# Moving statistics, weight loads and a write order in a two-layer convolution kernel on one core

## The chip, the cores and the metric

The kernel runs on one core of a Trainium2 chip. The metric is the device time of one execution in microseconds, as a median of several runs. Profiles are of one execution each; their spans start with the first instruction. Engines are named as the profile names them: PE (TensorE), DVE (VectorE), ACT (ScalarE), POOL (GpSimd), SP (the queue that issues most DMAs).

## The reference

The input x has four images of 16 channels and 256 x 256 pixels, float32. Two layers are added to it, each after a group normalization `_gn` (eight groups of two channels: subtract the mean, divide by the root of the variance plus 1e-5).

Layer 0 computes 400 = 16 x 25 logits per pixel by a 3 x 3 convolution of the normalized image, takes a softmax over the 25 of each channel, and uses these as weights for the 5 x 5 neighbours of the pixel in the normalized image:

```
out = conv(x_n, conv_w) + conv_b
weights = softmax(out.reshape(N, C, 25, H, W), axis=2)
x1 = x + sum over u of unfold(x_n)[:, :, u] * weights[:, :, u]
```

Layer 1 normalizes x1 in the same way, and adds to it a 3 x 3 convolution of silu of the normalized x1 and of eight cubic B-spline features of it, plus a bias. Layer 1 therefore needs the mean and variance of x1 for every image and group, which exist only when layer 0 has finished that image.

## The kernel before

**Prologue** (the code in the pool block before `layer0`). Each of the eight half images of x (128 rows, 16 channels) is loaded by `load_x` (the DMA at L413); the halves of image 0 stay in `held`. DVE takes statistics with bn_stats (L524, L526), ACT squares the same data (L533) and PE sums the squares (L536), for a bound on the logits. `group_stats` turns the statistics into mean and rstd; the power -0.5 is taken on POOL (L152, `rstd_x`), and DVE copies the result into `nrm[b]` (L544, L545), which holds rstd and -mean x rstd per group. Image 0 is then normalized by `normalize`, a generator that is advanced between the bn_stats of the later images: ACT writes normalized rows (L317, L330), PE transposes (L352), DVE and ACT write a plain copy, a rounded copy and the rest (L345, L360), and SP's queue writes all of that to scratch memory in HBM (`hs`, `hst`, `hsl`; the DMAs at L278 and L292). `normalize` first writes zero borders into that scratch (L250, L256, L257, twelve DMAs per image). The weights of both layers are loaded on SP's queue: `wr`, `wnr` (L421, L428, L433) for layer 0, and `sw`, `ss`, `bw` (L440, L442, L447: 27 + 3 + 1 DMAs) for layer 1. POOL multiplies sw by ss (L488) and rearranges `wr` and `wnr` (L465, L466). `norm_tiles` makes the buffers of `normalize` and clears them whole on POOL (L231, L233); it is called in the prologue and again in layer 0.

**Layer 0** goes over 64 strips of 128 rows x 32 columns, each in eight steps of four columns. In a step PE computes 400 logits for each column (L780, L784), ACT takes exp into `e[:, 0]` (L803), POOL multiplies with the neighbours into `e[:, 1]` (L808), and DVE sums both over the 25 neighbours into `nd` (L685): `nd[:, 0]` is the denominator and `nd[:, 1]` the weighted sum, both laid out column by column with the 16 channels innermost. There are four e buffers. A small scheduler, `after(k, f)` and `step()`, runs follow-up work k steps later: `seed` (ACT, Ln and Exp, L698 and L699), `divide` (DVE, L703 to L705, one Newton step in PSUM tile `r`), `apply` (POOL, L711: the weighted sum, which `divide` leaves with a minus sign, is subtracted from x in `xc`, which gives x1), and after every fourth strip `statistics` (DVE, eight bn_stats of 256 elements, L719) and `store` (a DMA on ACT's queue, L729). Beside the strips of images 0 to 2 the next image is normalized by `normalize`, one piece per step, on ACT, PE, DVE and SP's queue.

**Between the layers.** `scales(b)` turns the statistics of x1 (`st1[b]`) into the scale and bias of layer 1 for image b, in small steps on DVE, PE, ACT and POOL (L179 to L213). For images 0 and 1 these steps run in the last image of layer 0, for images 2 and 3 between units of layer 1.

**Layer 1** goes over 64 units of 16 rows. ACT makes distances and powers (L931, L161 to L164) and silu (L913), DVE the spline features (L156, L165 to L167) into `ring`, PE the convolution (L977, L985, L993), and DVE adds the bias (L960).

What sets the order: [...]The tile framework chooses the order from the order of the calls and from what each needs; `in_order` fixes it inside the layers, and `marks` lets the first work of layer 1 on ACT and SP slip between the last strips of layer 0, with the first silu (L913) behind all of layer 0's ACT work.

Of the kernel before, what the change touches and what calls it, by code (L numbers as in the profile page):

```python
# [11 lines left out]
F32 = mybir.dt.float32  # L12
F32R = mybir.dt.float32r
AF = mybir.ActivationFunctionType
ALU = mybir.AluOpType
AX = mybir.AxisListType
# [17 lines left out]
def conv_preact_kernel(  # L34
# [12 lines left out]
    nc = tc.nc  # L47
    B, C, H, W = x.shape
    G = 8
    GC = C // G  # L50
    P = 128
    NH = H // P
# [3 lines left out]
    PAD = K // 2  # L56
    HP = H + 2 * PAD
    NS = 8
    EPS = 1e-5
    SW = 32  # L60
# [3 lines left out]
    CX = 128  # L64
    JG = 4
    LAG = 1
    RP = P + 2
# [12 lines left out]
    const = ctx.enter_context(tc.tile_pool(name="const", bufs=1))  # L80
# [3 lines left out]
    hst = [[dram.tile([C, CT], F32, name=f"hst{b}_{h}") for h in range(NH)] for b in range(B)]  # L84
# [5 lines left out]
    ones = const.tile([P, P], F32, name="ones")  # L90
    nc.vector.memset(ones, 1.0 / P)
    mhalf = const.tile([P, G], F32, name="mhalf")
# [13 lines left out]
    gsel_sb = const.tile([P, G], F32, name="gsel_sb")  # L106
# [8 lines left out]
    KT = 6 * C + 1  # L115
# [9 lines left out]
    for r in range(RT):  # L125
        p = SROWS.index(r + 1) * C
# [1 line left out]

    edge = const.tile([P, 5], F32, name="edge")
    stat1 = ctx.enter_context(tc.tile_pool(name="stat1", bufs=1))  # L130
    st1 = [const.tile([P, G, NH * (W // CX), 6], F32, name=f"st1_{b}") for b in range(B)]

    def group_stats(pool, psum, st, name):

# [36 lines left out]
    def scales(b, psum):  # L171


        def small(n, name):
            return stat1.tile([P, n], F32, name=f"{name}_{b}", tag=f"{name}{b % 2}")

        mv = stat1.tile([P, G, 2], F32, name=f"mv_{b}", tag=f"mv{b % 2}")
        for g in range(G):
            nc.vector.bn_aggr(mv[:, g, :], st1[b][:, g].rearrange("p n s -> p (n s)"))  # L179
        yield  # L180
        ps = psum()[:, 0:G]
        nc.tensor.matmul(ps, lhsT=ones, rhs=mv[:, :, 0], start=True, stop=True)
        yield
        mean, d, rstd = small(G, "mean"), small(G, "d"), small(G, "rstd")
        q = stat1.tile([P, 6], F32, name=f"q_{b}", tag=f"q{b}")
        nc.vector.tensor_sub(d, mv[:, :, 0], ps)
        nc.vector.tensor_mul(mean, gsel_sb, ps)
        nc.vector.reduce_sum(q[:, 1:2], mean, AX.X)
        yield
        nc.scalar.activation(d, d, AF.Square)  # L190
        yield
        ps = psum()[:, 0:G]
        nc.tensor.matmul(ps, lhsT=ones, rhs=d, start=True, stop=False)
        nc.tensor.matmul(ps, lhsT=ones, rhs=mv[:, :, 1], start=False, stop=True)
        yield
        nc.vector.tensor_scalar(rstd, ps, EPS, None, ALU.add)  # L196
        yield
        nc.gpsimd.tensor_tensor(rstd, rstd, mhalf, ALU.pow)  # L198
        nc.gpsimd.tensor_mul(rstd, rstd, gsel_sb)
        yield  # L200
        nc.vector.reduce_sum(q[:, 0:1], rstd, AX.X)
        nc.vector.tensor_scalar(q[:, 1:2], q[:, 1:2], q[:, 0:1], -1.0, ALU.mult, ALU.mult)
        for k in range(2):
            nc.vector.tensor_scalar(q[:, 2 + k : 3 + k], q[:, k : k + 1], 2.5, None, ALU.mult)
        yield
        ps = psum()[:, 0:2]
        nc.tensor.matmul(
            ps, lhsT=sel.rearrange("p c s -> p (c s)"), rhs=q[0:C, 2:4], start=True, stop=True
        )
        yield  # L210
        nc.vector.tensor_copy(q[:, 4:5], ps[:, 0:1])
        nc.vector.tensor_add(q[:, 5:6], ps[:, 1:2], ub)
        sc[b] = tuple(q[:, k : k + 1] for k in (0, 1, 4, 5))  # L213
        yield
# [2 lines left out]


    nrm = [const.tile([P, 2, G], F32, name=f"nrm{b}") for b in range(B)]
    NIM = 3  # L220

    def norm_tiles(prep):


        xps = [prep.tile([P, QC, W + 2 * PAD], F32, name=f"xp{h}", bufs=1) for h in range(NH)]
        tts, his, los = [
            [prep.tile([P, NH, QG, RP], d, name=f"{v}{n}", bufs=1) for n in range(2)]
            for v, d in (("tt", F32), ("hi", F32R), ("lo", F32R))
        ]
        for t in (*tts, *xps):  # L230
            nc.gpsimd.memset(t, 0.0)  # L231
        for t in (*his, *los):
            nc.gpsimd.memset(t.bitcast(F32), 0.0)  # L233
        return prep, xps, tts, his, los

    zero = const.tile([PAD * C, max(RP, NST * SP)], F32, name="zero")
# [2 lines left out]
    zpad = const.tile([P, QC, PAD], F32, name="zpad")  # L239
    nc.vector.memset(zpad, 0.0)  # L240

    def normalize(b, ptr, tiles, held=None, copier=None):

        prep, xps, tts, his, los = tiles
        copier = copier or nc.scalar.copy
        for e in (0, HP - PAD):
            for r in range(PAD):
                nc.sync.dma_start(  # L250
                    hs[b][:, e + r].rearrange("s c w -> c s w"),
                    zero[0:C, 0 : NST * SP].rearrange("c (s w) -> c s w", s=NST),
                )
        for h in range(NH):
            for w in (0, (W + 1) * RP):
                nc.sync.dma_start(hst[b][h][:, w : w + RP], zero[0:C, 0:RP])  # L256
                nc.sync.dma_start(  # L257
                    hsl[b][h][:, :, w : w + RP].rearrange("c t r -> (c t) r"), zero[:, 0:RP]
                )

# [116 lines left out]
        for q in range(C // QC):  # L377
            ahead = rows(q + 1) if q + 1 < C // QC else iter(())
# [15 lines left out]
    with tc.tile_pool(name="prep0", bufs=2) as prep, tc.tile_pool(  # L394
        name="pre", bufs=1
    ) as pre, tc.tile_pool(
        name="xin", bufs=3
    ) as xin, tc.tile_pool(name="stat", bufs=2) as stat, tc.tile_pool(
        name="pstat", bufs=1, space=PSUM
    ) as pstat, tc.tile_pool(name="ptr0", bufs=3, space=PSUM) as ptr0:  # L400

        tiles = norm_tiles(prep)
        held = [pre.tile([P, C, W + 2 * PAD], F32, name=f"held{h}") for h in range(NH)]
# [15 lines left out]
        for dj in range(3):  # L419
            v = conv_wt[dj].rearrange("(d c) n -> c d n", d=3)  # L420
# [5 lines left out]
        v = conv_wt[2, 2 * C : 3 * C]  # L426
# [8 lines left out]
        sw = pre.tile([P, 3, 9, nm], F32, name="sw")  # L435
        ss = pre.tile([P, 3, 9, nm], F32, name="ss")
        for d in range(3):
            dc = slice(d * C, (d + 1) * C)
            for k in range(9):
                nc.sync.dma_start(sw[:, d, k], spl_w[dc, k])  # L440
            v = spl_s[dc]
            nc.sync.dma_start(  # L442
                ss[:, d],
                bass.AP(tensor=v.tensor, offset=v.offset, ap=[v.ap[0], [0, NS], [1, 9 * nm]]),
            )
        bw = pre.tile([nm, 9, nm], F32, name="bw")
        nc.sync.dma_start(bw, base_w)  # L447

        ups = pstat.tile([P, 1], F32, name="ups", tag="hps")
        nc.tensor.matmul(  # L450
            ups, lhsT=ubrow.rearrange("p c s -> p (c s)"), rhs=onec[0:1], start=True, stop=True
# [63 lines left out]
        ahead = iter(())  # L515
        for b in range(B):
            st = stat.tile([P, G, NH * (GC if b == 0 else 1), 6], F32, name=f"st0_{b}", tag=f"st0{min(b, 1)}")
            for hf in range(NH):
                n = b * NH + hf
                t = loaded.pop(0)  # L520
# [22 lines left out]
            mean, rstd = group_stats(stat, pstat, st, f"x{b}")  # L543
            nc.vector.tensor_copy(nrm[b][:, 0], rstd)  # L544
            nc.vector.scalar_tensor_tensor(nrm[b][:, 1], mean, -1.0, rstd, ALU.mult, ALU.mult)  # L545
            ms = stat.tile([P, 2], F32, name=f"ms_{b}", tag="ms")
            nc.vector.tensor_mul(mean, mean, mean)
            nc.vector.tensor_reduce(ms[:, 0:1], mean, AX.X, ALU.add)
# [8 lines left out]
            if b == 1:  # L557
                prepare1()
            if b == 0:
                ahead = normalize(0, ptr0, tiles, held, nc.vector.tensor_copy)  # L560
                next(ahead)
        for _ in ahead:
            pass
# [39 lines left out]
    def layer0(shift):  # L603
# [4 lines left out]
        with tc.tile_pool(name=f"prep{arm}", bufs=2) as prep, tc.tile_pool(  # L608
# [5 lines left out]
        ) as plog, tc.tile_pool(name=f"prc{arm}", bufs=1, space=PSUM) as prc:  # L614
            ans = [imp.tile([KT, CI * RP], F32R, name=f"an{n}{arm}", bufs=1) for n in range(NIM)]
            for t in ans:
                v = t.bitcast(F32)
                nc.vector.memset(v, 0.0)
                for r in (4 * C, 6 * C):
                    nc.vector.memset(v[r : r + 1], 1.0)  # L620
            tiles = norm_tiles(prep)
            strips = [(b, hf, s) for b in range(B) for hf in range(NH) for s in range(NST)]
            nci = SW // CI
# [49 lines left out]
            def after(k, f, *args):  # L673

                later.append([k, partial(f, *args)])
# [26 lines left out]
            def divide(n, nd, xc, r):  # L702
                nc.vector.tensor_mul(nd[:, 0], nd[:, 0], r)  # L703
                nc.vector.scalar_tensor_tensor(r, nd[:, 0], 2.0, r, ALU.subtract, ALU.mult)  # L704
                nc.vector.tensor_mul(nd[:, 1], nd[:, 1], r)  # L705
                after(LAG + 3, apply, n, nd, xc)

            def apply(n, nd, xc):
                w0 = strips[n][2] * SW % CX
                v = xc[:, :, w0 : w0 + SW]  # L710
                nc.gpsimd.tensor_sub(v, v, nd[:, 1].rearrange("p j c -> p c j"))  # L711
                if w0 + SW == CX:
                    after(2, statistics, n, xc)

            def statistics(n, xc):
                b, hf, s = strips[n]
                k = hf * (W // CX) + s * SW // CX
                for g in range(G):
                    nc.vector.bn_stats(  # L719
                        st1[b][:, g, k, :],  # L720
                        xc[:, g * GC : (g + 1) * GC, :].rearrange("p c w -> p (c w)"),
                    )
                after(2, store, n, xc)

            def store(n, xc):
                b, hf, s = strips[n]
# [104 lines left out]
    def layer1(arm, last, marks):  # L831
# [3 lines left out]
        with ExitStack() as pools:  # L835
# [135 lines left out]
            def outputs(n, sx):  # L971
# [27 lines left out]
                waiting.append((b, u, yp))  # L999

            more = chain(*(
                scales(b, lambda: pstat.tile([P, 8], F32, name=f"ps{arm}", tag="ps"))
                for b in range(2, B)
            ))
            for half in range(2):
# [90 lines left out]
```

## Time and profile before

| | us |
|---|---|
| three runs | 3112.22, 3113.82, 3114.83 |
| profiled execution | 3113.9, span 3112.0 |
| DVE busy | 3010.4 (97%) |
| PE busy | 2845.3 (91%) |
| ACT busy | 2083.5 (67%) |
| POOL busy | 1938.2 (62%) |

The prologue lasts to about 144 us, where the first product of layer 0 starts on POOL; layer 0 to about 2103 us, where DVE ends its last sum; the rest is layer 1. A share over the whole span mixes the three: POOL is at work in layer 0 and nearly idle in layer 1, ACT the other way round. Section 2 of the page shows it in 40 slices, each digit the busy tenths of some 78 us:

```profile
DVE  6689999999999999999999999999999999999997
ACT  6466655456564465555444444458999999999996
POOL 2289999999999999999999999990000001000000
```

A group of instructions reads as line, engine, operation, output and inputs, shape, number; then busy time and mean nanoseconds of one; then how long the engine idled ahead of it and what ended that.

### The profile page before, as it was taken

How to read it: one execution, taken by the hardware profiler on the slowest of the kernel's cores; microseconds unless marked ns; L12 is line 12 of the kernel's file. 1: busy time of each engine (PE TensorE's matmuls, PEld its weight loads, DVE VectorE, ACT ScalarE, POOL GpSimd, SP SyncE). 2: the span in 40 equal slices, each digit the busy share in tenths (PEclk: the TensorE clock that was granted, in tenths of full speed). 3: DMA queues.
4: the chain of work that ended last, by engine and by line, in shares of the span. 5: the costliest groups of instructions: out<-in, count | busy, mean ns of one | idle time of the engine just before them, and what ended most of it. 6: DMA issues, size and time to landing. Idle time of an engine off the chain costs nothing.

```text
span 3112.0 us, 40438 instructions
## 1 busy us (share of the span) xinstructions
PE 2845.3 (91%) x14776; PEld 1494.9 (48%) x14776; DVE 3010.4 (97%) x1733; ACT 2083.5 (67%) x2107; POOL 1938.2 (62%) x659
## 2 busy tenths in 40 slices
PE   3489999999999999999899999976999999999999
PEld 2356656656565566566565665641232223222222
DVE  6689999999999999999999999999999999999997
ACT  6466655456564465555444444458999999999996
POOL 2289999999999999999999999990000001000000
PEclk7699999999999999999999999998999999999999
DMA  7978878778877778788676666659999889999994
GB/s 222 309 206 232 241 207 224 194 212 223 239 218 214 204 198 234 215 223 231 186 192 168 167 177 180 166 135 199 193 196 195 197 193 192 194 196 197 193 197 92
DMA packets 356530, 626.34 MB, mean 201 GB/s; under 512 B 45298, under 2 KB 222692, under 8 KB 340452
## 3 DMA queue, kind: packets, MB, share of 16 engines
q1 hardware_dynamic: 323300, 606.88, 78.0%
q10 hardware_dynamic: 33024, 16.78, 1.9%
q8 instruction: 121, 1.98, 0.3%
q14 instruction: 85, 0.70, 0.1%
HBM read 513.95 MB, written 104.24 MB: 199 GB/s over the span
## 4 chain that ended last, share of the span: by engine, by line
DVE 69%; PE 11%; ACT 6%; issue 6%; DMA 5%; SPq 2%; POOL 0%; DVEq 0%; ACTq 0%; POOLq 0%
DVE nd L685 48%; PE lg L780 5%; PE yp L977 4%; DVE ta L166 3%; DVE ta L165 3%; DVE tb L166 3%; DVE tb L165 3%; DVE ring L167 2%; DMA xin<-in_x_dram 2%; PE lg L784 1%; DVE st L719 1%; DVE tb L156 1%; DVE r L704 1%; DMA sx<-x1s 1%; DVE nd L703 1%
## 5 line engine op out<-in xcount | busy, mean ns | idle before, releaser
L780 PE MATMUL lg<-wm,am 128*128 128x400 f32 x4096 | 1750.2, 508 | 122.5 <-ACT e L803 108.2
L808 POOL TENSOR_TENSOR e<-e,u 128x1600 f32<-128x1600 f32 x512 | 1788.8, 3536 | 69.4 <-ACT e L803 68.2
L685 DVE TENSOR_REDUCE nd<-e 128x128 f32<-128x3200 f32 x512 | 1747.5, 3476 | 23.3 <-POOL e L808 23.2
L803 ACT ACTIVATE e<-lg 128x800 f32<-128x800 f32 x1024 | 815.8, 836 | 896.6 <-DVE nd L685 762.7
L784 PE MATMUL lg<-wn,an 97*128 97x400 f32 x2048 | 1359.3, 664 | 0.1
L780 PEld LDWEIGHTS lg<-wm,am 128*128 128x128 f32 x4096 | 766.7, 194 | 449.4 <-ACT e L803 159.2
L977 PE MATMUL yp<-ring,wt 128*32 128x512 f32 x6144 | 737.9, 594 | 53.8 <-POOL ring L948 35.5
L784 PEld LDWEIGHTS lg<-wn,an 97*128 97x128 f32 x2048 | 391.1, 191 | 311.9 <-issue 15.7
L977 PEld LDWEIGHTS yp<-ring,wt 128*32 128x32 f32 x6144 | 210.9, 108 | 571.1 <-issue 454.0
L894 POOL MEMSET sx<- 16x256 f32 x8 | 2.4, 302 | 718.5 <-PE yp L985 278.6
L993 PE MATMUL yp<-sl,ws 64*32 64x512 f32 x1536 | 176.5, 588 | 0.0
L167 DVE SCALAR_TENSOR_TENSOR ring<-ta,ta 128x2048 f32<-128x2048 f32 (+1 forms) x64 | 147.9, 2310 | 2.5
L167 DVE SCALAR_TENSOR_TENSOR ring<-tb,tb 128x2048 f32<-128x2048 f32 x64 | 145.7, 2276 | 2.6
L166 DVE TENSOR_TENSOR ta<-ta,ta 128x2048 f32<-128x2048 f32 (+1 forms) x64 | 147.3, 2301 | 0.1
L166 DVE TENSOR_TENSOR tb<-tb,tb 128x2048 f32<-128x2048 f32 x64 | 145.3, 2271 | 0.0
L913 ACT ACTIVATE sl<-sx,q 64x2048 f32<-64x2048 f32 x64 | 133.5, 2085 | 0.3 <-DMA sx<-x1s 0.3
L164 ACT ACTIVATE ta<-ta 128x2048 f32<-128x2048 f32 (+1 forms) x64 | 123.2, 1925 | 2.0
L164 ACT ACTIVATE tb<-tb 128x2048 f32<-128x2048 f32 x64 | 120.5, 1883 | 0.8 <-POOL sx L894 0.6
L711 POOL TENSOR_TENSOR xc<-xc,nd 128x512 f32<-128x512 f32 x64 | 98.8, 1544 | 11.9 <-DVE nd L705 11.9
L198 POOL TENSOR_TENSOR rstd<-rstd,mhalf 128x8 f32<-128x8 f32 x4 | 7.5, 1866 | 158.0 <-DVE rstd L196 158.0
L993 PEld LDWEIGHTS yp<-sl,ws 64*32 64x32 f32 x1536 | 48.8, 106 | 116.2 <-issue 115.9
L931 ACT ACTIVATE xta<-xta,q 128x4096 f32<-128x4096 f32 (+4 forms) x23 | 83.7, 3640 | 0.0
(171 smaller groups left out, 1917.2 us busy)
## 6 DMA issues: line engine op xcount, KB each, us to landing
am<-hst SPq DMA_DIRECT2D x512, 194.6 KB
u<-hs SPq DMA_DIRECT2D x320, 288.0 KB
an<-hsl SPq DMA_DIRECT2D x512, 129.8 KB
xta<-x1s SPq DMA_DIRECT2D x40, 1024.0 KB
xtb<-x1s SPq DMA_DIRECT2D x40, 1024.0 KB
xtc<-x1s SPq DMA_DIRECT2D x40, 1024.0 KB
am<-hst SPq DMA_DIRECT2D x256, 129.8 KB
sx<-x1s SPq DMA_DIRECT2D x248, 128.0 KB
```

The source lines that it names most:

```text
L164: nc.scalar.activation(s1, r1, AF.Square, scale=2.0)
L165: nc.vector.scalar_tensor_tensor(s2, t, 2.0, s2, ALU.subtract, ALU.mult)
L166: nc.vector.tensor_mul(s1, s1, r1)
L167: nc.vector.scalar_tensor_tensor(f, s2, 0.0, s1, ALU.min, ALU.subtract if given else ALU.add)
L685: nc.vector.tensor_reduce(nd[:, :, j : j + JG, :], e.rearrange("p t j m c d -> p t j c m d"), AX.XY, ALU.add,)
L780: nc.tensor.matmul(lg[:, i, :NL], lhsT=am[:, o : o + P], rhs=wm.rearrange("p m c d -> p (m c d)"), start=True, stop=False,)
L784: nc.tensor.matmul(lg[:, i, :NL], lhsT=an[:, o : o + P], rhs=wn.rearrange("p m c d -> p (m c d)"), start=False, stop=True,)
L803: nc.scalar.activation(ev, lg[:, :, :NL], AF.Exp)
L808: nc.gpsimd.tensor_tensor(e[:, 1].rearrange("p j m c d -> p j (m c) d"), e[:, 0].rearrange("p j m c d -> p j (m c) d"), uv, ALU.mult,)
L913: nc.scalar.activation(sl[n % 2][:, :, 1 : W + 1], t, AF.Silu, scale=sc[b][0][0 : RD * C], bias=sc[b][1][0 : RD * C],)
L977: nc.tensor.matmul(yp[t * M : (t + 1) * M], lhsT=wt[:, d, e].rearrange("p r o -> p (r o)"), rhs=ring[:, r0 + t * RT + d : r0 + t * RT + d ...
L993: nc.tensor.matmul(yp[t * M : (t + 1) * M], lhsT=ws[:, e].rearrange("p r o -> p (r o)"), rhs=sl[n % 2][:, t : t + NT + 1 : NT, e : e + W], ...
```

## The change

Four things are changed together.

- `statistics` runs on ACT. In place of eight bn_stats on DVE it issues, for each of the eight groups, an Identity and a Square activation of the 256 elements with the group's scale and bias from `nrm`, each with an accumulated sum into `st1`. The eight groups are spread over eight steps, and `store` no longer waits for them. `scales` takes sums in place of bn_aggr results, with one matmul fewer and more of its small steps on POOL; a new tile `nrz` holds two constants for it, made in the prologue by one POOL and one DVE instruction per image.
- `divide` writes the weighted sum into a new tile `o`, channel by channel with the 32 columns innermost, and `apply` reads `o` as it lies.
- The loads of `sw`, `ss` and `bw`, and the zero borders of image 0, are issued on POOL's queue.
- `norm_tiles` clears only the borders of its buffers, and layer 0 sets only the rows of `an` that hold the constant 1 (three memsets on DVE in place of nine).

```diff
-    st1 = [const.tile([P, G, NH * (W // CX), 6], F32, name=f"st1_{b}") for b in range(B)]
+    NK = NH * W // CX
+    st1 = [const.tile([P, 2, G, NK], F32, name=f"st1_{b}") for b in range(B)]
...
-        mv = stat1.tile([P, G, 2], F32, name=f"mv_{b}", tag=f"mv{b % 2}")
-        for g in range(G):
-            nc.vector.bn_aggr(mv[:, g, :], st1[b][:, g].rearrange("p n s -> p (n s)"))
+        nc.vector.tensor_reduce(sums, st1[b].rearrange("p t g k -> p (t g) k"), AX.X, ALU.add)
         yield
-        ps = psum()[:, 0:G]
-        nc.tensor.matmul(ps, lhsT=ones, rhs=mv[:, :, 0], start=True, stop=True)
+        ps = psum()[:, 0 : 2 * G]
+        nc.tensor.matmul(ps, lhsT=ones, rhs=sums, start=True, stop=True)
...
+        nc.gpsimd.tensor_add(d, d, nrz[b][:, 1])
+        nc.gpsimd.tensor_tensor(p, d, mhalf, ALU.pow)
+        nc.gpsimd.tensor_mul(d, p, nrz[b][:, 0])
+        nc.gpsimd.tensor_mul(p, p, gsel_sb)
+        nc.gpsimd.tensor_mul(p, p, mz)
...
-        for t in (*tts, *xps):
-            nc.gpsimd.memset(t, 0.0)
-        for t in (*his, *los):
-            nc.gpsimd.memset(t.bitcast(F32), 0.0)
+        for t in xps:
+            nc.gpsimd.memset(t[:, :, 0:PAD], 0.0)
+            nc.gpsimd.memset(t[:, :, PAD + W :], 0.0)
+        for t in (*tts, *his, *los):
+            t = t if t.dtype == F32 else t.bitcast(F32)
+            nc.gpsimd.memset(t[:, 0, :, 0:1], 0.0)
+            nc.gpsimd.memset(t[:, NH - 1, :, RP - 1 :], 0.0)
...
-    def normalize(b, ptr, tiles, held=None, copier=None):
+    def normalize(b, ptr, tiles, held=None, copier=None, queue=nc.sync):
...
-                nc.sync.dma_start(
+                queue.dma_start(
                     hs[b][:, e + r].rearrange("s c w -> c s w"),
...
-                nc.sync.dma_start(sw[:, d, k], spl_w[dc, k])
+                nc.gpsimd.dma_start(sw[:, d, k], spl_w[dc, k])
...
-            nc.sync.dma_start(
+            nc.gpsimd.dma_start(
                 ss[:, d],
...
-        nc.sync.dma_start(bw, base_w)
+        nc.gpsimd.dma_start(bw, base_w)
...
+            nc.gpsimd.tensor_mul(nrz[b][:, 0], rstd, gsel_sb)
+            nc.vector.scalar_tensor_tensor(nrz[b][:, 1], rstd, EPS, rstd, ALU.mult, ALU.mult)
...
-                ahead = normalize(0, ptr0, tiles, held, nc.vector.tensor_copy)
+                ahead = normalize(0, ptr0, tiles, held, nc.vector.tensor_copy, nc.gpsimd)
...
-                nc.vector.memset(v, 0.0)
-                for r in (4 * C, 6 * C):
-                    nc.vector.memset(v[r : r + 1], 1.0)
+                nc.vector.memset(t.bitcast(F32)[4 * C : KT], 1.0)
...
-                nc.vector.tensor_mul(nd[:, 1], nd[:, 1], r)
-                after(LAG + 3, apply, n, nd, xc)
+                o = ndp.tile([P, C, SW], F32, name=f"o_{n}{arm}", tag="o", bufs=2)
+                nc.vector.tensor_mul(o.rearrange("p c j -> p j c"), nd[:, 1], r)
+                after(LAG + 3, apply, n, o, xc)
...
-                nc.gpsimd.tensor_sub(v, v, nd[:, 1].rearrange("p j c -> p c j"))
+                nc.gpsimd.tensor_sub(v, v, o)
                 if w0 + SW == CX:
-                    after(2, statistics, n, xc)
+                    for g in range(G):
+                        after(1 + g, statistics, n, xc, g)
+                    after(2, store, n, xc)
...
-                for g in range(G):
-                    nc.vector.bn_stats(
-                        st1[b][:, g, k, :],
-                        xc[:, g * GC : (g + 1) * GC, :].rearrange("p c w -> p (c w)"),
+                for t, f in enumerate((AF.Identity, AF.Square)):
+                    nc.scalar.activation(
+                        z, v, f, scale=nrm[b][:, 0, g : g + 1], bias=nrm[b][:, 1, g : g + 1],
+                        accum_out=st1[b][:, t, g, k : k + 1],
                     )
-                after(2, store, n, xc)
```

## The prediction

> **What bounds the kernel now.** I read three views in this order: busy time by stretch, groups of instructions, waits; then the order of time at the two seams. Stretches first (columns: stretch, length, then busy us and instructions of PE, PEld, DVE, ACT, POOL; clock, DMA share, GB/s):
>
> ```profile
> 31.00:107.50 76.50, 29.95 (x137) 23.86 (x136) 46.02 (x127) 54.11 (x83) 8.29 (x13) 0.61 0.74 224
> 155.00:2102.80 1947.80, 1818.57 (x6310) 1174.28 (x6310) 1928.04 (x903) 1043.87 (x1537) 1876.23 (x577) 0.98 0.75 203
> 2200.00:2300.00 100.00, 98.37 (x839) 29.20 (x835) 99.55 (x54) 99.56 (x50) 3.24 (x2) 1.00 0.93 194
> ```
>
> The first is the prologue: no engine is full. The second is layer 0: DVE is busy 1928.0 of 1947.8 us, POOL 1876.2, PE 1818.6, ACT only 1043.9. The third is layer 1: DVE and ACT are both full. Next the groups that the change touches:
>
> ```profile
> L808 POOL TENSOR_TENSOR e<-e,u 128x1600 f32<-128x1600 f32 x512 | 1788.8, 3536 | 69.4 <-ACT e L803 68.2 <-DMA u<-hs 1.0
> L685 DVE TENSOR_REDUCE nd<-e 128x128 f32<-128x3200 f32 x512 | 1747.5, 3476 | 23.3 <-POOL e L808 23.2
> L711 POOL TENSOR_TENSOR xc<-xc,nd 128x512 f32<-128x512 f32 x64 | 98.8, 1544 | 11.9 <-DVE nd L705 11.9
> L705 DVE TENSOR_TENSOR nd<-nd,r 128x512 f32<-128x512 f32 x64 | 43.9, 686 | 2.2
> L719 DVE BATCH_NORM_STATS2 st<-xc 128x6 f32<-128x256 f32 x128 | 43.2, 411 | 1.6 <-POOL xc L711 1.6
> ...
> L491 DVE TENSOR_REDUCE wc<-sw 128x48 f32<-128x432 f32 x3 | 2.4, 857 | 0.0
> ```
>
> L685 waited 23.3 us in all, five times, nearly all while layer 0 filled: DVE never starves later, so layer 0 lasts as long as DVE's sum. The waits say the same from the other side:
>
> ```profile
> ACT e L803 <- DVE nd L685: 762.7, 428, 6.5
> ...
> ACT e L803 <- PE lg L784: 121.7, 155, 10.8
> ...
> POOL e L808 <- ACT e L803: 68.2, 49, 13.3
> ```
>
> ACT waits for DVE to free an e buffer. In the prologue the chain of work runs over SP's queue: 31 weight DMAs, then zero fills, and only then the sixth load of x (L413), while DMA moves only 60 GB/s between 36 and 63 us (start us, us, what):
>
> ```profile
> 35.55 0.57 SPq L440
> ...
> 63.17 11.33 DMA xin<-in_x_dram
> ```
>
> At the seam of the layers, in order of time (start us, us, then the instruction and what its engine idled for):
>
> ```profile
> 2108.14 1.52 POOL L711 TENSOR_TENSOR xc<-xc,nd 128x512 f32<-128x512 f32 x1 [11.93 <-DVE nd L705]
> ...
> 2117.70 1.28 ACT L913 ACT_TABLE_LOAD   x1 [5.68 <-DMA x1s<-xc]
> ...
> 2131.07 2.28 DVE L166 TENSOR_TENSOR ta<-ta,ta 128x2048 f32<-128x2048 f32 x1
> ```
>
> [...]No write of this kind and length is in the trace. Its strided read is: L491 steps 48 words and takes 857 ns for 432 elements; a contiguous reduce of 256 (L539) takes 421, so 432 would take 421 + 176 x 1.04 = 604, and the stride costs 0.59 ns per element. [...]1544/512 = 3.0 ns per element at L711 (64-byte steps) against 3536/1600 = 2.2 at L808. [...]L317 (two pointers, 576 elements)[...] 863 in the trace. [...]No POOL DMA is in the trace.
>
> **The change part by part**, against the span of 3112.0 us; that execution took 3113.9, the three timed ones 3112.2 to 3114.8, so I apply the sum to the median 3113.8.
>
> *Statistics leave DVE.* 128 bn_stats go, 43.2 us. The last eight (2.7) belong to the seam below, so layer 0 gains **-40.5**: DVE is the bound, POOL and PE have 1876 and 1819 us of work against the 1887 that DVE keeps.
>
> *Statistics on ACT.* 16 groups of 128 columns x 8 channel pairs x 2 = 256 activations of 256 elements[...]; I take 0.6, up to 0.8 if the accumulator's read-out shows separately (no row). 154 us go into ACT's 1948 - 1044 idle. But they come in one strip of four, a pair per step: 16 x 0.8 (exp) + 9.6 + 1.2 (Ln, Exp) + about 4.2 (normalizing the next image) = 28 us of a strip of some 30. The first pair waits for POOL's subtraction; behind it in ACT's queue stand the next exps, for which POOL waits and whose logits' banks PE wants back. ACT is about a step ahead and regains that in the next three strips. **+3**, from 0 to +16 (a microsecond for each of 16 such strips).
>
> *Sums written by channel.* L705 now writes at 32-word steps. [...]**+21.6**[...]. POOL's subtraction falls from 1.54 to about 0.11 + 512 x 2.2 ns = 1.24 us, 19 us in all: worth nothing, as DVE never waits for POOL. The extra o buffers hold back no one, being freed by a subtraction a strip ahead.
>
> *Per-image scales.* Four images, each eight bn_aggr (1.11 us) for one reduce of 64 elements (about 0.25): with the fewer small steps some 0.9 each, on DVE in both layers, **-3.6**. POOL's three more small steps run beside its slack, or in layer 1 where POOL is idle.
>
> *The seam.* In the last strip nothing hides the statistics: 16 x 0.6 = 9.6 us on ACT after the last subtraction (about 2109.9), ahead of layer 1's three activations for tb (some 5.8, before at 2105.8 to 2112.0). The table load moves from 2117.7 to 2125.3, and ta L166 of the next unit from 2131.1 to about 2138. Layer 1 is full on both engines, so it stays: **+7** (to +10 at 0.8 us each). The store of x1, issued three steps earlier, is not last any more.
>
> *Prologue.* 31 weight DMAs (0.64 us apart on SP) and 12 zero fills of image 0 go to POOL: SP is free 25 us earlier. But by the program order of the changed kernel 36 of those 43 stand ahead of the first pow (L152) on POOL. That queue starts at some 3.3 us: sixteen memsets of the 0.12-us kind of L409 replace eight that ended at 9. [...]DVE's nrm copy and ACT's whole normalization wait on it. Load six then goes at about 41 + 8 (two row tiles on ACT) + 1 = 50, not 63; but the later loads stand on SP behind writes that come off ACT. ACT has 54.1 us of work from 31 to 107.5; with half of its 22 idle us it reaches the last Square at 41.4 + 54 + 11 = 106.4, before 107.5: **-1**. Ends: 0.64 us each (SP's pace) leaves rstd where it was and loads freed, -14; 1.5 us each, +17. sw x ss now stands ahead of the wm and wp copies; at about 55 us they still precede ACT's cast of wp. Memsets at the entry of layer 0: nothing, they end at 143.4 on POOL while u lands at 144.
>
> Sum: -40.5 + 3 + 21.6 - 3.6 + 7 - 1 = **-13.5**, so 3100.3 us.
>
> **Rivals.**
> - *The strided write eats the gain* (slower). Without it the sum is -35.1; shared by 64 writes that is 0.55 us, so above 1.07 ns per element extra the kernel loses.[...] For it: [...]ACT's own strided write (L330, 1323 ns for 512)[...]. Against: L491.
> - *The write is nearly free.* -35 gives 3079; DVE's 1887 is still the most, POOL having 1857. For it: a memset of 16 elements at 8-word steps (L97) takes 72 ns, eight adjacent ones (L93) 65.
> - *POOL's DMA queue holds rstd up.* At 1.5 us each the prologue gives +17 in place of -1: +4.5, 3118.[...] Against: SP's pace.
> - *ACT falls behind in the dense strips.* +16 in place of +3: 3113, no gain. Against: 763 us of waiting for DVE.
>
> **How the numbers follow.** Forecast (3088 to 3112) 0.42, strided write slow 0.20, write free 0.17, POOL queue 0.14, ACT dense 0.07. A measurement here tells 0.2% (6.2 us) from no change. Faster: nearly all of the forecast and the free write, 0.57. Slower: most of the slow write and over half of the queue, 0.23. Same: the rest, 0.20. The range takes in the free write and ends at the slow one: 3074 to 3126.
>
> **What would show it.** The write of o averages near 1.02 us (over 1.25 refutes the forecast); POOL's subtraction near 1.25; the statistics near 0.6 each and DVE still over 99% in layer 0; the first pow on POOL at about 39 us; sixth load near 50; table load of layer 1 some 16 us after the last subtraction. The forecast falls if DVE waits for POOL or ACT in layer 0, or layer 0 begins more than 10 us later.

## The result and the profile after

The changed kernel takes 3092.1 us (median of four runs, 3089.99 to 3093.62) against 3113.0 before: ratio 0.9932, 95% interval 0.9915 to 0.9949. That is -20.9 us where -13.5 was forecast. The profiled span is 3090.9 us (3112.0 before), so the two profiles show the same difference, -21.1.

The same three stretches as before, moved with the work (stretch, length, busy us of PE, PEld, DVE, ACT, POOL, then clock, DMA share, GB/s):

```profile
31.00:93.50 62.50, 32.87 (x143) 26.73 (x144) 50.61 (x139) 53.78 (x85) 13.99 (x24) 0.67 0.90 289
140.70:2067.60 1926.90, 1810.60 (x6302) 1166.67 (x6302) 1908.16 (x768) 1191.43 (x2016) 1861.55 (x583) 0.98 0.77 205
2200.00:2300.00 100.00, 98.11 (x848) 26.71 (x843) 99.52 (x58) 99.23 (x47) 6.69 (x4) 1.00 0.94 197
```

The prologue stretch ends with the start of the last Square on ACT, at 93.5 us in place of 107.5, and DMA moves 289 GB/s there in place of 224. Layer 0 is still DVE's, at 1908.2 of 1926.9 us. Layer 1 is full on both engines as before. The groups of instructions that were touched:

```profile
L691 DVE TENSOR_REDUCE nd<-e 128x128 f32<-128x3200 f32 x512 | 1746.9, 3476 | 31.6 <-POOL e L819 31.5
...
L731 ACT ACTIVATE z<-xc,nrm 128x256 f32<-128x256 f32 x256 | 153.6, 600 | 10.5 <-POOL xc L719 6.2
...
L719 POOL TENSOR_TENSOR xc<-xc,o 128x512 f32<-128x512 f32 x64 | 85.0, 1328 | 13.4 <-DVE o L713 13.4
...
L713 DVE TENSOR_TENSOR o<-nd,r 128x512 f32<-128x512 f32 x64 | 69.3, 1083 | 2.2
...
L731 ACT ACTIVATION_READ_ACCUMULATOR z<-xc,nrm 128x1 f32 x256 | 49.3, 192 | 0.0
```

The write of o takes 1083 ns (686 before), POOL's subtraction 1328 (1544), a statistic 600 ns, and the accumulator's read-out shows as an instruction of its own, 192 ns. The waits say that ACT has less to spare, but still some, and that DVE hardly waits:

```profile
ACT e L814 <- DVE nd L691: 522.3, 325, 4.8
ACT e L814 <- PE lg L795: 184.7, 198, 12.0
...
POOL e L819 <- ACT e L814: 48.6, 41, 11.1
DVE nd L691 <- POOL e L819: 31.5, 7, 17.3
```

Of DVE's 31.5 us, 29.4 lie in the first four waits, while layer 0 fills; 2.2 are left for the rest (1.1 before).

**Where the 21 us are.** I cut both traces at three marks: the third of the 512 big reduces (before it the waits of the fill end), the end of the last one, and the end of the second unit's features in layer 1. The first three rows are read off the order of time on DVE, the fourth is what is left of the span:

| | before | after | difference |
|---|---|---|---|
| to the third reduce | 168.2 | 153.9 | -14.4 |
| from there to the end of the last reduce | 1934.6 | 1913.8 | -20.8 |
| the seam: to the end of ring<-tb of unit 1 | 39.7 | 52.8 | +13.2 |
| the rest of layer 1 | 969.6 | 970.4 | +0.9 |

The forecast had -1, -40.5 + 3 + 21.6 - 1.8 = -17.7 and +7 for the first three. So the sum for the layer was about right, and two errors lie outside it, on opposite sides.

### The profile page after: what moved, and what is told of

The parts are those of the page before. It is cut to its first block, busy times and chain, and to the rows that moved or that the text cites. A ratio compares the mean times of both kernels' runs of the same rounds, so it can differ in the third digit from the quotient of the medians.

```text
span 3090.9 us, 40797 instructions
## 1 busy us (share of the span) xinstructions
PE 2840.5 (92%) x14760; PEld 1484.6 (48%) x14760; DVE 2976.4 (96%) x1571; ACT 2240.5 (72%) x2619; POOL 1951.1 (63%) x734
## 3 DMA queue, kind: packets, MB, share of 16 engines
q0 software_dynamic: 1472, 1.59, 0.2%
## 4 chain that ended last, share of the span: by engine, by line
DVE 65%; PE 9%; ACT 9%; issue 8%; DMA 6%; SPq 2%; POOL 1%; DVEq 0%; ACTq 0%; POOLq 0%
DVE nd L691 45%; PE yp L988 3%; PE lg L791 3%; DVE ta L169 3%; DVE ta L168 3%; DVE tb L169 3%; DVE tb L168 3%; DMA sx<-x1s 2%; DVE ring L170 2%; DVE o L713 1%; DVE tb L159 1%; DVE r L710 1%; DMA an<-hsl 1%; ACT sl L924 1%; ACT ta L167 1%
## 5 line engine op out<-in xcount | busy, mean ns | idle before, releaser
L691 DVE TENSOR_REDUCE nd<-e 128x128 f32<-128x3200 f32 x512 | 1746.9, 3476 | 31.6 <-POOL e L819 31.5
L795 PE MATMUL lg<-wn,an 97*128 97x400 f32 x2048 | 1349.7, 659 | 12.1 <-DMA an<-hsl 11.9
L795 PEld LDWEIGHTS lg<-wn,an 97*128 97x128 f32 x2048 | 389.3, 190 | 330.3 <-issue 21.1
L731 ACT ACTIVATE z<-xc,nrm 128x256 f32<-128x256 f32 x256 | 153.6, 600 | 10.5 <-POOL xc L719 6.2
L719 POOL TENSOR_TENSOR xc<-xc,o 128x512 f32<-128x512 f32 x64 | 85.0, 1328 | 13.4 <-DVE o L713 13.4
```

The costliest lines, as they stand in the source:

```text
L691: nc.vector.tensor_reduce(nd[:, :, j : j + JG, :], e.rearrange("p t j m c d -> p t j c m d"), AX.XY, ALU.add,)
L795: nc.tensor.matmul(lg[:, i, :NL], lhsT=an[:, o : o + P], rhs=wn.rearrange("p m c d -> p (m c d)"), start=False, stop=True,)
```

## The experiments

### One part at a time

The first run has the prologue part only (the queue and the fills); the second the statistics and scales only; the third the write by channel only, all on the kernel before, each with its hunks of the change's diff. Their cores, one after the other:

```diff
-                nc.sync.dma_start(sw[:, d, k], spl_w[dc, k])
+                nc.gpsimd.dma_start(sw[:, d, k], spl_w[dc, k])
```

```diff
-                    nc.vector.bn_stats(
+                    nc.scalar.activation(
```

```diff
-                nc.vector.tensor_mul(nd[:, 1], nd[:, 1], r)
+                nc.vector.tensor_mul(o.rearrange("p c j -> p j c"), nd[:, 1], r)
```

The fourth takes o out of the changed kernel:

```diff
-                o = ndp.tile([P, C, SW], F32, name=f"o_{n}{arm}", tag="o", bufs=2)
-                nc.vector.tensor_mul(o.rearrange("p c j -> p j c"), nd[:, 1], r)
+                nc.vector.tensor_mul(nd[:, 1], nd[:, 1], r)
...
-                nc.gpsimd.tensor_sub(v, v, o)
+                nc.gpsimd.tensor_sub(v, v, nd[:, 1].rearrange("p j c -> p c j"))
```

> The kernel before, with only the prologue part of the change: weight loads and image 0's zero fills on GpSimd's queue, narrow fills instead of whole-tile ones. Theory (the trace of the changed kernel shows the sixth load of x at 43.7 in place of 63.2 us, the eighth at 83.8 in place of 98.1, and layer 0's first transfer 13.8 us earlier): all of that comes from this part alone, -14 us, about 3099, with the eighth load again near 84. Rival A (the forecast's value): the freed queue is eaten again by writes that wait for ScalarE, -1 us, 3112; the 14 us would then need the other parts. Rival B: the head start is lost at the entry of layer 0, where the first strips wait for transfers: -3 to -7 us.

> The kernel before, with only the statistics on ScalarE and the scales that go with them; sums written and subtracted as before, prologue as before. Theory: VectorE loses 40.5 us of bn_stats in layer 0 and about 2 us of scale steps and stays the engine that sets layer 0; the seam costs 13 us, as in the changed kernel: -29 us, 3084, and GpSimd's busy time in layer 0 does not decide. Rival A (GpSimd takes over as the bound, with its strided subtraction at 1.54 us it has 1876 us against VectorE's 1886): layer 0 gains only about 25 us, total -12, 3101, with VectorE waiting for GpSimd at the big reduce more than 30 us beyond the fill. Rival B (ScalarE's dense strips hold the others up): -13 or less, with waits of GpSimd for the exp.

> The kernel before, with only the weighted sums written by channel into a tile of their own. Theory: 64 writes 0.40 us longer each, all on VectorE, which sets layer 0: +25 us, 3138, the write averaging 1.08 us and GpSimd's subtraction 1.3 us. Rival (the faster subtraction gives GpSimd's slack back to VectorE's waits): +10 or less.

> The changed kernel, with the weighted sums written pixel by pixel and read at steps by GpSimd, as before. Theory: the write by channel costs 25 us on VectorE and buys nothing: about 3067 us, 25 faster than the changed kernel. Rival (GpSimd's 0.22 us more per strip, 14 us in all, now make GpSimd the bound, or its step and VectorE's meet more often): 3080 to 3092, with VectorE waiting for GpSimd at the big reduce.

| | us | ratio to before, 95% | first part | layer 0 |
|---|---|---|---|---|
| prologue only | 3101.6 | 0.9956 (0.9942 to 0.9969) | -12.1 | +0.1 |
| statistics only | 3093.0 | 0.9932 (0.9919 to 0.9946) | +1.6 | -35.8 |
| o only | 3132.1 | 1.0058 (1.0044 to 1.0072) | +0.9 | +17.5 |
| changed without o | 3079.2 | 0.9886 (0.9871 to 0.9901) | -12.9 | -36.0 |

The last two columns are the first two differences of the table above, from each run's trace. (The kernel before took 3114.6 us beside these runs.) The three parts alone sum to a ratio of 1 - 0.0044 - 0.0068 + 0.0058 = 0.9946; together they give 0.9932, within the intervals.

The prologue part is worth 13 us by itself; the forecast's -1 falls. The statistics alone bring the time to 3093.0 where I expected 3084: layer 0 gained some 7 us less than the 42.5 that I had counted, and the seam cost the 13 us that were in the expectation. The write costs 17.5 us, not the 25 that I expected from its longer duration, and taking it out gives 14 (0.9932 - 0.9886 = 0.0046) rather than 25; at 3079.2 that run is next to its rival's 3080 to 3092. Two things are behind the write's lower cost, and both can be read. First, the duration overstates what the engine is held. In order of time on DVE, the write and the instruction behind it, in the changed kernel:

```profile
920.53 1.05 DVE L713 TENSOR_TENSOR o<-nd,r 128x512 f32<-128x512 f32 x1
921.45 0.66 DVE L366 TENSOR_TENSOR lo<-tp,hi 128x512 fp32r<-128x512 f32 x1
```

and in the kernel before:

```profile
941.11 0.69 DVE L705 TENSOR_TENSOR nd<-nd,r 128x512 f32<-128x512 f32 x1
941.72 0.68 DVE L360 TENSOR_TENSOR lo<-tp,hi 128x512 fp32r<-128x512 f32 x1
```

Start to start it is 0.92 us against 0.61: the next instruction starts 0.14 to 0.18 us before the slow write's recorded end, and 0.08 before the end of the fast one. Over the 63 writes ahead of the last the mean from start to start is 0.923 us against 0.605. So a write holds DVE 0.32 us longer, 63 x 0.318 = 20.0 us in layer 0. Second, without o the strided read on POOL does cost something once DVE has lost its bn_stats. Groups of the run with statistics only:

```profile
L690 DVE TENSOR_REDUCE nd<-e 128x128 f32<-128x3200 f32 x512 | 1748.7, 3477 | 28.0 <-POOL e L816 27.9
...
L716 POOL TENSOR_TENSOR xc<-xc,nd 128x512 f32<-128x512 f32 x64 | 102.8, 1606 | 9.2 <-DVE nd L710 9.2
```

Most of these 27.9 us are the waits of the fill. Behind the third reduce DVE waits 6.3 us for POOL here and 5.8 in the changed kernel without o, against 3.2 in the changed kernel and 2.1 in the kernel before. At three of the four longest of these waits in this run (1.5, 1.2 and 1.0 us) the subtraction stands just ahead of the product that DVE waits for. With DVE at 1888 us of work in layer 0 and POOL at 1873 they meet now and then: neither rival (POOL or ACT as the bound, -12) holds, but some 3 us of the gain go to it. The write's cost then adds up. With o only, DVE spends 20.0 us more on the writes, waits 1.1 us less for POOL, and its 510 big reduces are 1.4 us shorter in sum: 17.5. On top of the rest it is 20.2 - 2.6 - 2.4, the 15.2 between the last row and the changed kernel. Why the reduces are a little shorter beside the faster subtraction, no run shows.

### How the write pays

Two layouts of o in the changed kernel: pairs of channels side by side, and channel rows 33 words apart.

```diff
-                o = ndp.tile([P, C, SW], F32, name=f"o_{n}{arm}", tag="o", bufs=2)
-                nc.vector.tensor_mul(o.rearrange("p c j -> p j c"), nd[:, 1], r)
+                o = ndp.tile([P, C // 2, SW, 2], F32, name=f"o_{n}{arm}", tag="o", bufs=2)
+                nc.vector.tensor_mul(
+                    o.rearrange("p h j k -> p j h k"),
+                    nd[:, 1].rearrange("p j (h k) -> p j h k", k=2),
+                    r.rearrange("p j (h k) -> p j h k", k=2),
+                )
...
-                nc.gpsimd.tensor_sub(v, v, o)
+                nc.gpsimd.tensor_sub(
+                    v.rearrange("p (h k) j -> p h k j", k=2), v.rearrange("p (h k) j -> p h k j", k=2),
+                    o.rearrange("p h j k -> p h k j"),
+                )
```

```diff
-                o = ndp.tile([P, C, SW], F32, name=f"o_{n}{arm}", tag="o", bufs=2)
+                o = ndp.tile([P, C, SW + 1], F32, name=f"o_{n}{arm}", tag="o", bufs=2)[:, :, 0:SW]
```

> The changed kernel, with o laid out by pairs of channels: VectorE writes two adjacent words, then hops 64 words; GpSimd reads at steps of two words. Theory (the extra time is paid by each single-word hop, and two adjacent words are written at full rate): the write is back at 0.69 us, start to start 0.61, and the 15 us that layer 0 lost to the write come back: 3076 to 3079; GpSimd's subtraction stays at 1.3 to 1.35 us, so a few us of VectorE's waits for GpSimd may go too, down to 3073. Rival A (each hop costs, half as many hops): 0.87 us, 3085. Rival B (GpSimd's read at two words costs like its read at 16): subtraction 1.55 to 1.6 us, 3079 as without o.

> The changed kernel, with o's channel rows 33 words apart in place of 32. Theory (a single-word hop costs whatever its step): write at 1.08 us as before, 3092. Rival (the 32-word step hits the same part of the memory each time): write at 0.69 to 0.8 us, 3077 to 3083.

Pairs: 3074.8 us, ratio 0.9878 (0.9863 to 0.9893). Rows of 33 words: 3096.8, ratio 0.9949 (0.9933 to 0.9964), no better than the changed kernel. In the groups of the pair layout,

```profile
L723 POOL TENSOR_TENSOR xc<-xc,o 128x512 f32<-128x512 f32 x64 | 85.4, 1335 | 11.0 <-DVE o L713 11.0
...
L713 DVE TENSOR_TENSOR o<-nd,r 128x512 f32<-128x512 f32 x64 | 44.1, 688 | 2.2
```

the write is back at 688 ns and POOL's read at steps of two words stays at 1335, like the contiguous one. With rows of 33 words the write takes 1109 ns, against 1083 at 32 and 688 in pairs: it is the hop after every single word that costs here, not the 32-word step. Layer 0 is 18.0 us shorter than in the changed kernel. It is also 2.8 shorter than without o, where only POOL's subtraction is slower: that is what the faster subtraction is worth here. From start to start, single-word hops of 32 words lose 0.32 us / 512 = 0.62 ns per element (0.66 at 33 words), and pairs none.

### The seam

In the changed kernel, in order of time over all engines (start us, us):

```profile
2064.13 3.48 DVE L691 TENSOR_REDUCE nd<-e 128x128 f32<-128x3200 f32 x1
...
2073.32 3.42 POOL L719 TENSOR_TENSOR xc<-xc,o 128x512 f32<-128x512 f32 x1 [13.36 <-DVE o L713]
2075.55 3.60 DVE L169 TENSOR_TENSOR ta<-ta,ta 128x2304 f32<-128x2304 f32 x1
...
2076.78 0.60 ACT L731 ACTIVATE z<-xc,nrm 128x256 f32<-128x256 f32 x1 [6.04 <-POOL xc L719]
...
2087.39 1.16 SPq L895 DMA_DIRECT2D xtb<-x1s  x2
...
2087.45 2.56 DVE L170 SCALAR_TENSOR_TENSOR ring<-ta,ta 128x2304 f32<-128x2304 f32 x1 [8.29 <-ACT z L731]
...
2093.06 1.28 ACT L924 ACT_TABLE_LOAD   x1
...
2099.55 3.81 ACT L942 ACTIVATE xtb<-xtb,q 128x4096 f32<-128x4096 f32 x1 [3.09 <-DMA xtb<-x1s]
...
2103.39 1.23 DVE L159 TENSOR_SCALAR tb<-xtb 128x2048 f32<-128x2048 f32 x1 [5.56 <-ACT xtb L942]
```

and in the kernel before:

```profile
2102.79 1.16 SPq L884 DMA_DIRECT2D xtb<-x1s  x2
...
2120.99 3.79 ACT L931 ACTIVATE xtb<-xtb,q 128x4096 f32<-128x4096 f32 x1
```

The last reduce ends at 2067.61 in the changed kernel and at 2102.76 before. The tile xtb takes the rows of x1 for layer 1's second unit.

The table load comes 16.3 us after POOL's last subtraction, as forecast. But three things act on ACT's way to its activation on xtb, not one. That activation starts 31.9 us after the last reduce, where it started after 18.2: 13.7 later, about the 13.2 of the table.

- The subtraction ends 9.1 us after the last reduce, where it ended after 6.9: 2.2 us. This one takes 3.42 us, against a median of 1.29. With bn_stats gone, DVE goes straight on to layer 1 beside it.
- From there to the table load it is 16.3 us in place of 8.0: 8.3 us. The sixteen activations with their read-outs take 10.6 us (2076.78 to 2087.37), with the three for tb behind them; before, ACT waited 5.7 of the 8.0 us for the store of x1.
- The load of xtb is issued only as the last statistic ends, 19.8 us after the last reduce, where it went with the last reduce before. ACT waits 3.1 us for it.

DVE feels it as two waits, 8.3 us for the last statistic before it can write ring and 5.6 us for ACT's activation on xtb. All this fits xtb and ring lying where the z tiles were, which take the output of the statistics that nobody reads. That I inferred from these releases; two runs test it, both on the changed kernel without o. One gives the last strip back to bn_stats, and turns the result into sums in layer 1, when image 3 is due:

```diff
+                if n == len(strips) - 1:
+                    nc.vector.bn_stats(tail[:, g, :], v)
+                    return
...
+        if b == B - 1:
+            mv = stat1.tile([P, G, 2], F32, name="mv", tag="mv")
+            for g in range(G):
+                nc.vector.bn_aggr(mv[:, g, :], tail[:, g, :])
+            yield
+            nc.gpsimd.tensor_mul(mz, mv[:, :, 0], nrm[b][:, 0])
...
+            for t, v in ((0, mz), (1, p)):
+                nc.vector.tensor_scalar(
+                    st1[b][:, t, :, NK - 1], v, float(GC * CX), None, ALU.mult
+                )
```

The other only moves the z tiles into memory of their own:

```diff
+    zs = [const.tile([P, GC * CX], F32, name=f"z{k}") for k in range(2)]
...
-                z = l0.tile([P, GC * CX], F32, name=f"z_{n}_{g}{arm}", tag="z")
+                z = zs[g % 2]
```

> The changed kernel without o, and with the very last strip's statistics taken by VectorE's bn_stats, turned into sums four fifths into layer 1 (8 bn_aggr and small steps). Against the changed kernel without o (3079.2, ratio 0.9886 to before). Theory: the seam loses the 10.6 us of 16 activations on ScalarE and with them the late release of the z tiles, for which the load of xtb waits (issued 19.8 us after the last reduce in the changed kernel, at once in the kernel before); it is charged 2.7 us of bn_stats and about 1.5 us of steps on VectorE later: -9 us, 3070, ratio near 0.9857; xtb's load issued with the last reduce. Rival A (only the activations' time counts, the load is late for another reason): -6, with ScalarE still waiting for xtb. Rival B (layer 1 takes up the delay of its start): 0.

> The changed kernel without o, and with the two z tiles that the statistics write in memory of their own, so that no buffer of layer 1 lies where they were; the last strip's statistics stay on ScalarE. It splits the 13 to 15 us that moving them to VectorE gave (ratio 0.9886 without, 0.9843 with). Theory: the load of xtb is issued with the last reduce again and ScalarE no longer waits for it; that part is worth 3 to 6 us (ratio 0.9868 to 0.9876), the 10.6 us of activations themselves the rest. Rival A (the activations are all of it): 0 to -1 us. Rival B (the late load is most of it): -9 us or more.

Last strip on DVE: 3063.6 us, ratio 0.9843 (0.9829 to 0.9856); z apart: 3071.7, ratio 0.9866 (0.9851 to 0.9881), at the edge of the 0.9868 to 0.9876 that I expected; both against 0.9886 without either. From the last reduce to the end of unit 1's features it is 53.1 us without either, 45.7 with z apart, 39.0 with the last strip on DVE. With z apart, in order of time:

```profile
2051.22 1.16 SPq L894 DMA_DIRECT2D xtb<-x1s  x2
...
2062.84 2.58 DVE L171 SCALAR_TENSOR_TENSOR ring<-ta,ta 128x2304 f32<-128x2304 f32 x1
```

The load goes at once (the last reduce ends at 2051.19), DVE writes ring without a wait, and ACT puts two of the three activations for tb ahead of the statistics, where it had stood waiting for the subtraction. It was the tile's memory, and it held more than the load. So of 14 us, 7.4 were the late release and 6.7 the activations and the slowed subtraction. The run with the last strip on DVE:

```profile
2058.27 1.16 SPq L913 DMA_DIRECT2D xtb<-x1s  x2
...
2063.62 1.52 POOL L734 TENSOR_TENSOR xc<-xc,nd 128x512 f32<-128x512 f32 x1 [9.23 <-DVE nd L728]
...
2065.18 2.71 DVE L746 BATCH_NORM_STATS2 tail<-xc 128x6 f32<-128x256 f32 x8 [1.63 <-POOL xc L734]
```

POOL's subtraction is at 1.52 us again, with DVE waiting for it. The seam is as short as in the kernel before (39.0 against 39.7 us), so all of its loss is back, where I had expected -9: I had counted the activations and the load, and not the subtraction, and had charged 1.5 us for steps later in layer 1 that don't show there (969.5 us against 970.3 without this).

### The prologue

One more run on the kernel before has the DMAs on POOL's queue, but the wide fills:

```diff
-                ahead = normalize(0, ptr0, tiles, held, nc.vector.tensor_copy)
+                ahead = normalize(0, ptr0, tiles, held, nc.vector.tensor_copy, nc.gpsimd)
```

and the queue of `sw`, `ss` and `bw` as above.

> The kernel before, with the 43 DMAs on GpSimd's queue but the fills as wide as before. Theory (the gain is the sixth load of x, freed from SP's queue): nearly all of the prologue part's 13 us, -11 to -13, about 3102; the wide fills at the entry of layer 0 are hidden, but GpSimd starts its queue 6 us later, so the first pow comes 3 to 6 us later than in the run with narrow fills and up to 3 us may be lost. Rival (the narrow fills carry it): -5 or less.

It takes 3099.6 us, ratio 0.9958 (0.9944 to 0.9971), the same as the whole prologue part (0.9956). The queue carries it; the narrow fills are worth nothing that can be measured. Which of the DMAs on the queue carry it, the 31 weight loads or the 12 zero fills, no run separates; in the kernel before they took SP from 35.6 to 56.4 us and from there to 62.0. In the changed kernel, in order of time over all engines:

```profile
2.50 4.40 POOL L446 DMA_DIRECT2D sw<-in_spl_w_dram  x8
8.38 0.52 POOL L446 DMA_DIRECT2D sw<-in_spl_w_dram  x1 [1.48 <-DMA sw<-in_spl_w_dram]
...
30.02 0.51 POOL L262 DMA_DIRECT2D hst<-zero  x1 [0.56 <-DMA sw<-in_spl_w_dram]
32.51 1.68 POOL L155 TENSOR_TENSOR rstd_x<-var_x,mhalf 128x8 f32<-128x8 f32 x1 [1.97 <-DVE var_x L153]
...
43.72 1.34 SPq L419 DMA_DIRECT2D xin<-in_x_dram  x1
...
93.46 3.62 ACT L539 ACTIVATE xq<-xin 128x4096 fp32r<-128x4096 f32 x1
```

Each of the first eight DMAs takes POOL 0.55 us. They go back to back, later ones wait for earlier ones to land; 36 of them, with waits, lie between 2.50 and 30.5 us, 0.78 us each. Then POOL waits 1.97 us for DVE: the queue does not hold the pow up. The first rstd is there at 34.2 us all the same, 3.5 later than in the kernel before, because DVE starts on the first load of x 1.2 us later (11.70 against 10.47) and waits 1.86 us for the third. The sixth load goes at 43.7 (63.2 before), the last Square on ACT starts at 93.5 (107.5).

### Together, and one step further

> The changed kernel with o laid out by pairs and the last strip's statistics on VectorE. Theory: the two gains lie at different places and add: 0.9878 - 0.0043 = 0.9835, 3061 us, faster than both kernels and than either alone. Rival: with GpSimd's slack used up the pair layout's 3 us over no o at all are gone, 0.9843.

Pairs and the last strip on DVE: 3061.3 us, ratio 0.9830 (0.9817 to 0.9844); the two gains add, and this is faster than both kernels by 53 and 31 us. The last run adds a hold of four steps on image 1's normalization once its first load is issued, because ACT waits for this load in all these kernels (14.8 us before, 12.3 in the run above):

```diff
-                    next(ahead, None)
+                    if n > 0 or not 0 < j <= 4 * JG:
+                        next(ahead, None)
```

> The same, with the normalization of image 1 held back by four steps after its first load is issued, so that the activation that waits for this load (13 us in every kernel here, with the first strips' exps queued behind it on ScalarE) is emitted later. Theory: most of VectorE's 11.6-us wait at its third reduce goes: -8 to -11 us, near 3051. Rival A (the first strips wait for their own transfers then): -3 or less. Rival B (the held-back steps come due all at once before the last strip of image 0): no gain or a loss.

3058.5 us, ratio 0.9823 (0.9809 to 0.9836): 3 us by the medians, not 8 to 11, and the intervals overlap. In order of time over all engines, a new wait has taken the place of the old one: the third reduce comes 10.1 us earlier, and the rest of layer 0 takes 6.1 us longer.

```profile
154.36 1.67 PE L818 MATMUL lg<-wm,am 128*128 128x400 f32 x2 [4.15 <-DMA am<-hst]
...
158.19 0.84 ACT L841 ACTIVATE e<-lg 128x800 f32<-128x800 f32 x1 [6.34 <-PE lg L822]
...
165.48 3.49 DVE L708 TENSOR_REDUCE nd<-e 128x128 f32<-128x3200 f32 x1 [7.03 <-POOL e L846]
```

PE now waits for its own im2col load `am`, ACT for PE, and DVE for POOL at the seventh reduce: rival A.

## Why the forecast came out right, and what was wrong in it

The sign and most of the size hold: the profile's reading that DVE sets layer 0, that its bn_stats come off its time and that a strided write gives part of that back is what the runs show one by one. That the total is so near is in part luck. Against the forecast the prologue is off by -13.4 us, layer 0 by -3.1, the seam by +6.2 and the rest of layer 1 by +2.7. Within layer 0 two errors cancel as well: the statistics gained some 3.4 us less and the write cost 6.4 less than forecast.

Of the signs that I gave, the statistic's length (0.60 us), DVE's share of layer 0 (1908.2 of 1926.9, 99.0%), POOL's subtraction (a median of 1.29) and the table load (16.3 us behind the last subtraction) came as said. The write (1.08 us for 1.02), the first pow (32.5 us for 39) and the sixth load (43.7 for 50) did not.

- **Statistics on ACT, layer 0**: forecast -40.5 + 3, and -1.8 of scales, -39.3; measured -35.8. Read off DVE in the run with statistics only: the bn_stats free 39.3 us from start to start (40.5 is the sum of their durations) and the small steps 2.2, but DVE waits 4.2 us more for POOL, and its big reduces are 1.3 us longer in sum. So the +3 for crowding was near in size, but the longest waits have another reason than ACT's dense strips: most of them come behind POOL's subtraction. I had called POOL free because DVE never waited for it before, which was true of DVE's 1928 us, not of 1888. How much of the rest is ACT's crowding stays open: in the pair layout, with the faster subtraction, 4.0 us of such waits are left against 2.1 before.
- **The strided write**: forecast +21.6; measured +17.5 alone and +15.2 on top of the rest (layer 0 with and without o). The term rested on my estimate of a price per element that the trace of before did not show, and so did the slow end of the range. The strided read L491 gave 0.59 ns, with 1.04 ns per contiguous element, which the trace of before has between ring<-ta,ta of 2304 and of 2048 elements, (2561 - 2294) / 256. DVE was held 0.62. The step that failed is that POOL's faster subtraction is "worth nothing": the pair layout shows it at 2.8 us. Its size was also less than 3.0 against 2.2 ns per element, L711 against L808, suggests: like against like, the strided read takes a fifth more (a mean of 1.54 us in the kernel before, of 1.28 with o only). The check I gave, a mean near 1.02 us, read 1.08, and the mean overstates the cost by a quarter (0.40 us against 0.32).
- **Statistic's length**: 0.6 us, as forecast; the read-out adds 0.19 but two neighbours overlap, so sixteen take 10.6 us, 0.66 each.
- **Scales**: forecast -3.6. DVE's small steps in layer 0 take 2.2 us less, about as forecast for that half; in layer 1 nothing of it shows (+0.9).
- **The seam**: forecast +7, measured +13.2. Its own term, the table load 7.6 us later behind the subtraction, was near (8.3). Missing were the memory that a new tile takes from layer 1's first buffers, and that DVE, no longer held by the last subtraction, slows it. For the second the traces show both sides: beside DVE's ta<-xta,ta and ta<-ta,ta the subtraction took 3.42 us, and of the two ta<-ta,ta took 3.60, 2.55 before. Where DVE stood waiting, in the run with the last strip on DVE, the subtraction took 1.52 us and ta<-ta,ta 2.56.
- **Prologue**: forecast -1, measured -12 to -14, the end that I gave for 0.64 us per DMA. The step that failed is the first rstd at 41 us: it took 36 us for 36 DMAs on POOL's queue, a pace that was my estimate and that no trace had shown. It was 0.55 us each, 0.78 with the waits, and rstd was there at 34.2, so ACT's normalization began at 34.6 and not at 41.4. The second is "half of its 22 idle us": ACT's work from there to the last Square was about as counted (53.2 us), but its idle time only 5.7 us and not 11, since the loads that it had waited for come earlier. The two make up 12.1 of the 12.9 us between 106.4 and 93.5.

Of the rivals, the slow write falls (0.62 ns per element, where 1.07 was the point of decision), the free write too, POOL's queue holding rstd up too (1.97 us of waiting for DVE), and the dense strips on ACT were a few us at most, not 16.

## What to carry to other kernels

Work moved off the busiest engine loses part of its worth as that engine comes near the next one's load (here some 4 of 40 us, with DVE at 1888 us and POOL at 1873), so compare the loads after the change, not before. A step that is hidden a hundred times is bare at the end of its stage: price the last one by itself, with the memory its tiles take from the next stage and the engine it no longer holds back. Where a layout must be turned, try runs of two words: here the write took 688 ns, as before the turn (686), and the reader a mean of 1335, as on contiguous data (1328).

## What the runs showed of the hardware

- An activation with an accumulated sum leaves two instructions, here 0.60 us and 0.19 us for 256 elements; sixteen such pairs in a row took 10.6 us, 0.66 each.
- A DMA issued by POOL held it 0.49 to 0.59 us (one of 43 took 0.74), for 8 to 216 KB; eight went in a row in 4.40 us, then POOL waited 1.48 us for an earlier one to land.
- A DVE write of 512 elements cost 0.62 ns more per element when it hopped 32 words after every word and 0.66 at 33 words, and nothing more when it hopped 64 words after every pair (688 ns against 686).
- POOL's subtraction of 512 elements took, in the median, 1.54 us (before) and 1.59 (changed without o) at 16-word steps and 1.29 contiguous (changed); at two-word steps the mean was 1.335, against 1.328 contiguous, with the one at the seam in both. At the seam, beside DVE's ta<-xta,ta and ta<-ta,ta, it took 3.42 us (changed) and 3.77 (statistics only, changed without o, z apart), with DVE waiting for it 1.52 (before, and the last strip on DVE).
- The recorded duration of the slow write overlaps the next instruction's by 0.14 to 0.18 us, that of the fast one by 0.08; from start to start they are 0.923 and 0.605 us.
